# A graph network kernel: the scatters of its result are put behind the last gather of sources in POOL's order

## The chip, the cores and the metric

The kernel runs on one core of a Trainium2 chip. The metric is device microseconds (us) of one execution: the median of several runs, lower is better. Engines are named as the profile names them: PE (matmuls), PEld (its weight loads), DVE (vector), ACT (scalar), POOL and SP. POOL and SP also issue DMA transfers; each engine takes its instructions in the order in which they stand in its own queue.

## What is computed

Two layers of a graph network over 6250 nodes with 128 features and 206250 edges, each with a residual and a layer norm. Here is the reference cut to its frame:

```python
x = layernorm(x + L0(x))      # 5 rounds of h = segment_sum(h[col] * w, row), then a linear layer
x = layernorm(x + L1(x))      # attention of every node over its incoming edges:
#   k, v  = (x[src] * (edge_sh @ Wang.T)) @ Wlin * (relu(edge_attr @ W1 + b1) @ W2)
#   alpha = <q[dst] Wdot, k> per head;  attn = softmax of alpha over the edges of one dst
#   L1    = segment_sum(attn * v, dst) @ Wout
```

The second layer is the part that the change touches.

## The kernel before

The first part of the program sorts and counts edges and runs the five rounds of the first layer as matmuls with a matrix of counts (`propagate`). It leaves the first layer's result twice in DRAM: `x1_d` in the order of nodes, and `x1_r` in the order of rank, where nodes are ranked by how many edges they have. That makes 49 tiles of 128 nodes each, and tile `t` needs at most `WIDTHS[t]` edges per node: 64 for the first tile, 22 for the last, 1658 in all.

`attend` (line 709) is the second layer. A tile's edges are taken as columns: column `j` holds edge `j` of each of its 128 nodes. Up to four columns make a group, and there are 433 groups. For a group:

- `fetch` (line 764) brings in what it needs. For each column one indirect DMA, issued from POOL (line 782), gathers the 128 source rows of 512 bytes from `x1_d` into the tile `xs`; `xs` has six buffers, one per group. SP's queue loads edge data (`ea`, line 775) and, once per tile, the nodes' own rows (`x1s`, line 768).
- `turn`, `nets`, `radial` and `keys` (lines 806 to 870) are the compute: transposes of `xs` (line 811) and matmuls on PE, copies out of PSUM on ACT, products on DVE.
- After a tile's last group, `softmax` (line 872) runs as a generator. It is stepped a little at a time between the groups that follow, and ends with the tile's result `z[:, t, :]` and its mean and variance.
- After the tiles numbered 12, 25, 38, 45, 47 and 48 (`NORMS`, line 47) the layer norm of all tiles since the last such point is finished: one DVE instruction per tile (line 927) and behind it one indirect DMA from POOL (line 931), which scatters the tile's 128 rows to their nodes' places in `out`.

The loop (line 947) goes over `i`, the group now in the nets, and fetches group `i + 3` at its top. The order of PE, DVE and ACT is the order of the program text as it runs (`manual_schedule`, line 946). POOL and SP are not in that list: a planner places their instructions, by its estimates of when their inputs are ready. `declare_no_dep` says that two scatters need not wait for each other. After `attend` the program loads a flag (`flag2`, line 1269) on every engine and, in this case, branches past a general version of the work.

Of the kernel before, what the change touches and what calls it, by code (L numbers as in the profile page):

```python
# [18 lines left out]
P = 128  # L19
N = 6250  # L20
# [123 lines left out]
def stats(nc, work, z, v):  # L144
    st = work.tile([P, nc.vector.BN_STATS_DIM], F32, name="st")
    nc.vector.bn_stats(st, z)
    nc.vector.bn_aggr(v, st)
# [528 lines left out]
def pieces(t):  # L676

    return [(c, OFFS[t] + c * SC, min(SC, WIDTHS[t] - c * SC)) for c in range(-(-WIDTHS[t] // SC))]
# [30 lines left out]
def attend(tc, w1, b1, wang, w2, wlin, wqd, wout, ident, rows, c_iota, src_all, eas_o, x1_d, x1_r, out):  # L709


    nc = tc.nc
    WM = WIDTHS[0]
    with ExitStack() as s:
        one = s.enter_context(tc.tile_pool(name="at1", bufs=1))
# [30 lines left out]
        nc.vector.tensor_scalar(none, degf, 0.0, None, OP.is_equal)  # L746
        z = one.tile([P, NT, D], F32, name="z")
        v = one.tile([P, NT, 2], F32, name="v2")
        puts = []
        kvs = [one.tile([P, WIDTHS[i], DK + D], F32, name=f"kv{i}") for i in range(2)]  # L750

        groups = [(t, j, min(4, w - j)) for t, w in enumerate(WIDTHS) for j in range(0, w, 4)]
# [3 lines left out]
        def ps(name):  # L756
            return pp.tile([P, CH], F32, name=name, tag="ps")
# [6 lines left out]
        def fetch(g):  # L764
            t, j, n = groups[g]
            if j == 0:
                x1s[t] = three.tile([P, D], F32, name="x1s")
                nc.sync.dma_start(x1s[t], x1_r[t * P:(t + 1) * P, :])
            if j % SC == 0:

                c, s, m = pieces(t)[j // SC]
                ea[t, c] = three.tile([P, 4, SC * 32], FR, name="ea")
                for i in range(8):
                    at = (i % 4 // 2) * 32 + i // 4 * 16
                    nc.sync.dma_start(
                        ea[t, c][16 * i:16 * i + 16, :, :m * 32].bitcast(F32),
                        bass.AP(tensor=eas_o.tensor, offset=eas_o.offset + (at * OFFS[NT] + s) * P,
                                ap=[[OFFS[NT] * P, 16], [m * 32, 4], [1, m * 32]]))
            xs[g] = deep.tile([P, 4, D], F32, name="xs")
            for i in range(n):  # L780
                c = OFFS[t] + j + i
                nc.gpsimd.indirect_dma_start(  # L782
                    out=xs[g][:, i, :], out_offset=None, in_=x1_d[:, :],
                    in_offset=bass.IndirectOffsetOnAxis(ap=src_all[:, c:c + 1], axis=0))

        def begin(t):

# [49 lines left out]
        def radial(g):  # L837

            t, j, n = groups[g]
            r = r1.pop(g)  # L840
            p_r = pp.tile([P, 2, CH], F32, name="p_r")
            for i in range(n):
                u = i % 2 * (DK + D)
                nc.tensor.matmul(p_r[:, i // 2, u:u + DK + D], r[:, i, :], w2_s, start=True, stop=True)  # L844
            rr[g] = two.tile([P, 4, DK + D], F32, name="rr")
            r2 = rr[g].rearrange("p (b i) f -> p b (i f)", i=2)
            for b, f in banks(n):
                nc.scalar.copy(r2[:, b, :f], p_r[:, b, :f])  # L848

        def keys(g):  # L850
# [12 lines left out]
            for b, f in banks(n):  # L863
# [5 lines left out]
            nc.vector.tensor_reduce(al[t][:, j:j + n], a[:, :, :DK].rearrange("p j (h k) -> p j h k", h=H),  # L869
                                    AX.X, OP.add)  # L870

        def softmax(t):

            w = WIDTHS[t]
            a = kv[t]
            l = al.pop(t)[:, :w]
            ex = two.tile([P, WM, H], F32, name="ex")
            m = two.tile([P, H], F32, name="m")
            d = two.tile([P, H], F32, name="d")
            nc.vector.tensor_tensor(l, l, keep[t][:, :w, None].to_broadcast([P, w, H]), OP.min)  # L880
            nc.vector.tensor_reduce(m, l.rearrange("p j h -> p h j"), AX.X, OP.max)
            nc.vector.tensor_tensor(l, l, m[:, None, :].to_broadcast([P, w, H]), OP.subtract)
            yield
            nc.scalar.activation(ex[:, :w], l, AF.Exp)
            yield
            nc.vector.tensor_tensor(ex[:, :w], ex[:, :w],
                                    ok[t][:, :w, None].to_broadcast([P, w, H]), OP.mult)
            nc.vector.tensor_reduce(d, ex[:, :w].rearrange("p j h -> p h j"), AX.X, OP.add)
            nc.vector.tensor_scalar(d, d, none[:, t:t + 1], None, OP.add)
            nc.vector.reciprocal(d, d)  # L890
            yield

            for u in range(0, w, 8):
                k = min(8, w - u)
                av = a[:, u:u + k, DK:].rearrange("p j (h f) -> p j h f", h=H)
                nc.vector.tensor_tensor(av, av, ex[:, u:u + k, :, None].to_broadcast([P, k, H, D // H]),  # L896
                                        OP.mult)
                yield
                if u > 0:
                    nc.vector.tensor_add(a[:, :k, DK:], a[:, :k, DK:], a[:, u:u + k, DK:])  # L900
                    yield
            for h in (4, 2, 1):
                nc.vector.tensor_add(a[:, :h, DK:], a[:, :h, DK:], a[:, h:2 * h, DK:])  # L903
            yield
            av = a[:, :1, DK:].rearrange("p j (h f) -> p j h f", h=H)
            o = two.tile([P, H, D // H], F32, name="o")
            nc.vector.tensor_tensor(o, av[:, 0], d[:, :, None].to_broadcast([P, H, D // H]), OP.mult)
            yield
            tr = ps("tr4")
            nc.tensor.transpose(tr[:, :P], o.rearrange("p h d -> p (h d)"), ident)  # L910
            oT = two.tile([P, P], F32, name="oT")
            nc.scalar.copy(oT, tr[:, :P])
            yield
            y = ps("y4")
            nc.tensor.matmul(y[:, :D], oT, wo, start=True, stop=True)
            nc.vector.tensor_add(z[:, t, :], x1s.pop(t), y[:, :D])
            stats(nc, two, z[:, t, :], v[:, t, :])
            if t + 1 in NORMS:
                yield
                t0 = NORMS[NORMS.index(t + 1) - 1]  # L920
                rs = two.tile([P, NT], F32, name="rs")
                n = t + 1 - t0
                nc.vector.tensor_scalar(rs[:, :n], v[:, t0:t + 1, 1], EPS, None, OP.add)
                nc.scalar.activation(rs[:, :n], rs[:, :n], AF.Sqrt)
                nc.vector.reciprocal(rs[:, :n], rs[:, :n])
                for u in range(t0, t + 1):
                    nc.vector.tensor_scalar(z[:, u, :], z[:, u, :], v[:, u, 0:1],
                                            rs[:, u - t0:u - t0 + 1], OP.subtract, OP.mult)

                    k = min(P, N - u * P)  # L930
                    st = nc.gpsimd.indirect_dma_start(
                        out=out[:, :], in_=z[:k, u, :], in_offset=None,
                        out_offset=bass.IndirectOffsetOnAxis(ap=rows[:k, u, 0:1], axis=0)).ins
                    for q in puts:
                        tc.declare_no_dep(st, q, reason="a node has one place in the order")
                    puts.append(st)
                    if u % 4 == 3:
                        yield

# [2 lines left out]
        def step(of):  # L942
            if of and next(of[0], None) is None and of[0].gi_frame is None:
                of.pop(0)

        with tc.manual_schedule(engines=MANUAL):
            for i in range(-3, len(groups) + 1):
                live = [0 <= i + x < len(groups) for x in range(-1, 4)]
                if live[4]:
                    fetch(i + 3)  # L950
                if live[1]:
                    nets(i)
                step(running)
                if live[0]:
                    radial(i - 1)
                if live[2]:
                    turn(i + 1)
                step(running)
                if live[0]:
                    keys(i - 1)  # L960
                    t, j, n = groups[i - 1]
                    if j + n == WIDTHS[t]:
                        running.append(softmax(t))
                if len(running) > 1:
                    step(running)
                if live[3] and groups[i + 2][1] == 0:
                    begun.append(begin(groups[i + 2][0]))
                step(begun)
            for r in running:
                for _ in r:  # L970
                    pass


def attend_any(tc, w1, b1, wang, w2, wlin, wqd, wout, c_heads, c_sum, ident, last, srct, dstt, eat,
# [375 lines left out]
```

## Time and profile before

| | us |
|---|---|
| median of 3 runs | 4537.38 (4534.1 to 4539.81) |
| the profiled execution, its own time | 4539.91 |
| its span in the trace | 4538.1 |
| first gather of line 782 starts | 2248.5 |
| first scatter of line 931 starts | 3049.5 |
| last gather of line 782 starts | 4489.4 |
| last scatter of line 931 starts | 4525.3 |

Between 2248 and 4490 us, a stretch of 2242 us, the engines' busy times are PE 1934.84, PEld 1770.90, DVE 1931.95, ACT 893.28 and POOL 1721.02 us, with a granted PE clock of 0.96 of full speed and the DMA engines busy for 0.53 of the time.

How to read the profile: a busy time is the sum of the durations of an engine's instructions, and leaves out the instructions that only handle registers, branches and semaphores. A line "L782" is line 782 of the kernel. In a group of instructions the first number after the bar is the busy time, the second the mean duration of one in ns, and after the second bar stands how long the engine idled just before these instructions and what ended most of that idle time ("issue" is time in which the engine waited for nothing that the profile shows). In a wait, the three numbers are the total, the number of times and the longest.

### The profile page before, as it was taken

Reading aid. Unit: us, or ns where it says so; the run is one execution under the profiler, and the core shown is the slowest. Engines: PE = TensorE matmul, PEld = TensorE weight load, DVE = VectorE, ACT = ScalarE, POOL = GpSimd, SP = SyncE. Lnnn points to the kernel's source line nnn. Section 1 sums busy time; section 2 is a strip of 40 time slices with the busy share of each in tenths; the row PEclk is TensorE's granted clock in tenths of the full one; section 3 lists DMA queues with packets and bytes.
Section 4 is the critical chain, followed back from the end, with each engine's and each line's share of the span. In section 5 each row is a group of like instructions: output and inputs, shape, how many; then the busy total and the mean of one; then the engine's idle time right before and its main releaser. Section 6 shows DMA issues by size and latency. Waiting matters only on the chain.

```text
span 4538.1 us, 73113 instructions
## 1 busy us (share of the span) xinstructions
PE 3783.3 (83%) x24823; PEld 3370.0 (74%) x24823; DVE 3762.0 (83%) x6000; ACT 2045.8 (45%) x4137; POOL 2361.9 (52%) x2339
## 2 busy tenths in 40 slices
PE   4455666988999999999698888988888878888886
PEld 4455555877888888887488888877878878787775
DVE  9899997757877778766479888997888979898897
ACT  0156665545556565554243434443434434444343
POOL 0350000264333434312477777777777777777774
PEclk9966777999999999999899999999999999999998
DMA  9033335557777788755365555554555555555442
GB/s 325 11 81 80 79 80 139 139 145 217 230 230 220 224 248 239 229 154 161 102 111 102 100 103 105 101 98 97 101 99 102 100 106 98 105 104 102 93 101 46
DMA packets 389736, 601.64 MB, mean 133 GB/s; under 512 B 120093, under 2 KB 325205, under 8 KB 378554
## 3 DMA queue, kind: packets, MB, share of 16 engines
q1 hardware_dynamic: 255930, 356.57, 32.4%
q0 software_dynamic: 127056, 204.67, 19.8%
q10 hardware_dynamic: 6368, 35.63, 2.3%
q8 instruction: 201, 3.29, 0.3%
q14 instruction: 181, 1.48, 0.1%
HBM read 491.89 MB, written 132.25 MB: 138 GB/s over the span
## 4 chain that ended last, share of the span: by engine, by line
PE 22%; DVE 10%; DMA 8%; POOL 8%; issue 6%; ACT 1%; SPq 0%; POOLq 0%; DVEq 0%; ACTq 0%
DMA xs<-x_d,src_all 8%; POOL xs L782 7%; PE p_r L844 6%; PE p_k L860 5%; PE p_k L858 3%; PE acc L438 3%; DVE mkv L833 3%; DVE kv L865 3%; PE p_g L825 2%; PE p_x L811 1%; DVE kv L896 1%; PE p_h L825 1%; DVE kv L903 1%; DVE kv L867 1%; POOL x_r L362 1%
## 5 line engine op out<-in xcount | busy, mean ns | idle before, releaser
L782 POOL DMA_INDIRECT xs<-x_d,src_all x1658 | 1674.0, 1010 | 507.0 <-issue 431.3
L438 PE MATMUL acc<-c,parts 128*128 128x512 f32 (+1 forms) x6370 | 1410.0, 382 | 53.9 <-DVE c L421 40.0
L438 PEld LDWEIGHTS acc<-c,parts 128*128 128x128 f32 x6370 | 1154.1, 189 | 280.0 <-DVE c L421 44.9
L421 DVE CAST c<-c 128x1024 fp32r<-128x1024 uint8 x980 | 683.6, 716 | 251.6 <-PE acc L438 186.4
L860 PE MATMUL p_k<-wlin_s,mkv 128*128 128x128 f32 x3316 | 756.5, 311 | 0.0
L434 ACT CAST c<-c 128x512 fp32r<-128x512 uint8 x735 | 454.8, 621 | 559.2 <-PE acc L438 434.6
L858 PE MATMUL p_k<-wlin_s,mkv 128*128 128x64 f32 x3316 | 582.5, 259 | 66.7 <-DVE kv L865 65.7
L844 PE MATMUL p_r<-w_s,r 128*128 128x192 f32 x3316 | 618.9, 329 | 0.0
L858 PEld LDWEIGHTS p_k<-wlin_s,mkv 128*128 128x128 f32 x3316 | 524.4, 199 | 96.8 <-DVE kv L865 96.0
L844 PEld LDWEIGHTS p_r<-w_s,r 128*128 128x128 f32 x3316 | 569.1, 193 | 34.0 <-ACT rr L848 0.2
L865 DVE TENSOR_TENSOR kv<-rr,p_k 128x768 f32<-128x768 f32 (+2 forms) x443 | 396.7, 897 | 205.8 <-PE p_k L860 189.8
L848 ACT COPY rr<-p_r 128x768 f32<-128x768 f32 (+2 forms) x443 | 334.8, 758 | 475.0 <-PE p_r L844 465.0
L833 DVE TENSOR_TENSOR mkv<-p_g,xT 128x512 f32<-128x512 f32 (+3 forms) x866 | 533.9, 658 | 7.1 <-PE p_g L825 6.7
L860 PEld LDWEIGHTS p_k<-wlin_s,mkv 128*128 128x128 f32 x3316 | 524.6, 199 | 0.0
L827 ACT ACTIVATE r<-p_h,b_s 128x512 f32<-128x512 f32 (+3 forms) x433 | 289.9, 670 | 461.4 <-PE p_h L825 454.7
L223 PE MATMUL p_c<-oh_h,oh_l 128*128 128x100 bf16 x3136 | 301.2, 273 | 214.8 <-DVE oh_h L153 214.8
L662 POOL DMA_DIRECT2D eas_o<-eT_l x252 | 204.1, 813 | 504.7 <-DVE eT_l L656 490.4
L223 PEld LDWEIGHTS <-oh_l 128*128 128x128 bf16 x3136 | 289.5, 124 | 223.5 <-DVE oh_h L153 216.9
L811 PE MATMUL p_x<-ident,xs 128*128 128x128 f32 x1658 | 277.0, 279 | 130.8 <-DMA xs<-x_d,src_all 123.8
L225 ACT CAST cT<-p_c 128x500 uint8<-128x500 f32 (+1 forms) x637 | 306.3, 638 | 61.3 <-DVE c_row L231 61.2
L811 PEld LDWEIGHTS p_x<-ident,xs 128*128 128x128 f32 x1658 | 212.5, 142 | 163.4 <-DMA xs<-x_d,src_all 127.5
L814 ACT COPY xT<-p_x 128x512 f32<-128x512 f32 (+3 forms) x433 | 247.9, 573 | 136.8 <-PE p_x L811 134.0
(195 smaller groups left out, 4533.7 us busy)
## 6 DMA issues: line engine op xcount, KB each, us to landing
c<-counts SPq DMA_DIRECT2D x360, 384.0 KB
ea<-eas_o SPq DMA_DIRECT2D x648, 128.0 KB
c<-counts SPq DMA_DIRECT2D x120, 448.0 KB
eas_o<-eT_l POOLq DMA_DIRECT2D x162, 256.0 KB
counts<-c_row SPq DMA_DIRECT2D x582, 48.0 KB
xs<-x_d,src_all POOLq DMA_INDIRECT x1658
eat<-in_eas ACTq DMA_DIRECT2D x1, 25792.0 KB
counts<-c_row SPq DMA_DIRECT2D x194, 56.0 KB
```

Of the source, the lines that this page charges most:

```text
L223: nc.tensor.matmul(p_c[:, q - q0], oh_los[t % 2][:, q // Q, :, q % Q], oh_hi[:, q // Q, :, q % Q], start=True, stop=True)
L421: nc.vector.tensor_copy(c[:, u:u + 1024].rearrange("p (n b x) -> p n b x", n=2, b=2), r[:, :, v:v + 512].rearrange("p b (n x) -> p n b x", ...
L434: nc.scalar.copy(c[:, 1024:w].rearrange("p (b x) -> p b x", b=2), r[:, :, 512:])
L438: nc.tensor.matmul(a[:, :v - u], parts[:, j, i, :], c[:, u:v], start=(j == 0 and i == 0), stop=(j == NT - 1 and i == 1))
L782: nc.gpsimd.indirect_dma_start(out=xs[g][:, i, :], out_offset=None, in_=x1_d[:, :], in_offset=bass.IndirectOffsetOnAxis(ap=src_all[:, c:c ...
L811: nc.tensor.transpose(p_x[:, i * P:(i + 1) * P], xs[g][:, i, :], ident)
L833: nc.vector.tensor_tensor(mkv[g][:, i, :n].rearrange("p j (b e) -> p b j e", b=4), p_g[:, i, :n * P].rearrange("p (b j e) -> p b j e", b=4 ...
L844: nc.tensor.matmul(p_r[:, i // 2, u:u + DK + D], r[:, i, :], w2_s, start=True, stop=True)
L848: nc.scalar.copy(r2[:, b, :f], p_r[:, b, :f])
L858: nc.tensor.matmul(p_k[:, i // 2, u:u + DK], m[:, 0, i, :], wlin_s[:, :DK], start=True, stop=True)
L860: nc.tensor.matmul(p_k[:, i // 2, u + DK:u + DK + D], m[:, 1, i, :], wlin_s[:, DK:], start=True, stop=True)
L865: nc.vector.tensor_mul(k.rearrange("p (b i) f -> p b (i f)", b=b.stop - b.start), r2[:, b, :f], p_k[:, b, :f])
```

## The change

The scatter leaves `softmax`. There, `done` now only notes that a tile is normed. A new function `store` issues the scatters of all tiles in `done`, each within `tc.issue_after(fetched)`, which gives POOL's order an edge from the instruction `fetched` to each scatter: the scatter stands behind it in the queue, without a semaphore to wait for. `fetched` is what `fetch` returns, the last gather of the group fetched last. `store` is called only from the point in the loop at which no group is left to fetch, and in the loop that runs the remaining generators to their end. The scatters keep their order among themselves, their inputs and their destinations.

```diff
-        puts = []
+        puts, done = [], []
...
-                nc.gpsimd.indirect_dma_start(
+                fetched = nc.gpsimd.indirect_dma_start(
                     out=xs[g][:, i, :], out_offset=None, in_=x1_d[:, :],
-                    in_offset=bass.IndirectOffsetOnAxis(ap=src_all[:, c:c + 1], axis=0))
+                    in_offset=bass.IndirectOffsetOnAxis(ap=src_all[:, c:c + 1], axis=0)).ins
+            return fetched
...
+        def store():
+
+            for u in done:
+
+                k = min(P, N - u * P)
+                with tc.issue_after(fetched):
+                    st = nc.gpsimd.indirect_dma_start(
+                        out=out[:, :], in_=z[:k, u, :], in_offset=None,
+                        out_offset=bass.IndirectOffsetOnAxis(ap=rows[:k, u, 0:1], axis=0)).ins
+                for q in puts:
+                    tc.declare_no_dep(st, q, reason="a node has one place in the order")
+                puts.append(st)
+            done.clear()
...
-                    k = min(P, N - u * P)
-                    st = nc.gpsimd.indirect_dma_start(
-                        out=out[:, :], in_=z[:k, u, :], in_offset=None,
-                        out_offset=bass.IndirectOffsetOnAxis(ap=rows[:k, u, 0:1], axis=0)).ins
-                    for q in puts:
-                        tc.declare_no_dep(st, q, reason="a node has one place in the order")
-                    puts.append(st)
+                    done.append(u)
...
-                    fetch(i + 3)
+                    fetched = fetch(i + 3)
...
+                if i + 3 >= len(groups):
+                    store()
             for r in running:
                 for _ in r:
-                    pass
+                    store()
+                store()
```

## The prediction

> **What bounds the kernel now.** I began with the page's busy row in 40 slices. From slice 20 on, which is about 2248 us and the start of `attend`, PE, PEld and DVE stand at 7 to 9 tenths and POOL at a flat 7. Nothing there is full, so I asked the groups by line what the idle time before POOL's work is.
>
> ```profile
> POOL 0350000264333434312477777777777777777774
> L782 POOL DMA_INDIRECT xs<-x_d,src_all x1658 | 1674.0, 1010 | 507.0 <-issue 431.3
> ```
>
> The gathers of sources (line 782) are busy 1674.0 us, and POOL idled 507.0 us before them: 0.306 us before each of the 1658. That is a fixed gap, not a wait. The timeline of POOL shows it, here at the last block of scatters and on to the end of the program:
>
> ```profile
> 4475.37 0.97 POOL L931 DMA_INDIRECT out<-z,rows  x1 [0.31 <-DMA out<-z,rows]
> 4476.64 0.97 POOL L931 DMA_INDIRECT out<-z,rows  x1 [0.30 <-issue]
> 4477.92 0.99 POOL L782 DMA_INDIRECT xs<-x_d,src_all  x1 [0.30 <-PE p_h L825]
> ...
> 4488.13 0.95 POOL L782 DMA_INDIRECT xs<-x_d,src_all  x1 [0.30 <-issue]
> 4489.39 0.95 POOL L782 DMA_INDIRECT xs<-x_d,src_all  x1 [0.31 <-issue]
> 4511.42 1.10 POOL L931 DMA_INDIRECT out<-z,rows  x1 [21.07 <-DVE z L927]
> 4512.82 0.99 POOL L931 DMA_INDIRECT out<-z,rows  x1 [0.30 <-DVE al L882]
> 4525.33 1.57 POOL L931 DMA_INDIRECT out<-z,rows  x1 [11.51 <-DVE z L927]
> ```
>
> Columns: start, duration, then in brackets the idle time before. Whatever the bracket names, the gap is 0.30. From the first gather (2248.5) to the end of the last (4490.3) POOL issues 1658 gathers and 46 scatters in one unbroken row; three gaps of 1703 are over 0.4 us, the longest 0.94. So POOL never waits for a free `xs` buffer, though only six exist: the compute always keeps up, and **POOL's rate of issue sets the length of the stage**, although its busy share is 7 tenths. The other side of it is PE's waits between 2248 and 4490:
>
> ```profile
> PE p_x L811 <- DMA xs<-x_d,src_all: 123.8, 80, 8.1
> PE p_k L858 <- DVE kv L865: 62.5, 99, 1.6
> ```
>
> PE stood 123.8 us waiting for gathered sources, its largest wait in the stage.
>
> **What is removed from the middle.** 46 scatters (tiles 0 to 45) stand ahead of the last gather, in blocks near 3049, 3663, 4202 and 4466; three come after it. In the groups of the window 2248 to 4491 the 46 are busy 47.2 us with 14.0 us of gaps before them: 61.2 us, 1.33 per slot. With them gone every later gather is issued sooner, and the last one ends at 4490.3 - 61.2 = **4429.2**.
>
> Does the compute follow? Yes, by a comparison inside the trace: between the blocks POOL already runs gathers alone (2300 to 3045, 3085 to 3660, 3700 to 4200, 4235 to 4463), and in each of these PE still waits for sources: 32.1, 32.2, 12.0 and 10.6 us. Those stretches are what the whole stage becomes. SP's loads (`ea`, `x1s`) follow as they do there.
>
> **What is added at the end.** The 46 scatters go behind the last gather, on the same engine and DMA queue. No engine waits for a scatter's landing except the end of the program, so nothing but scatters 47 to 49, the load of `flag2` (0.33 us on POOL's queue) and the end stands behind them. Their data are long there. Price of a slot: 1.33 (the mean of the 46, beside compute) or 1.27 (0.97 + 0.30, the quiet ones). I take 1.33, since half of the train still runs beside the last tiles: 46 x 1.33 = 61.2, so POOL is at 4429.2 + 61.2 = 4490.3. POOL's total work until here is only reordered; the gain is not in it.
>
> **Where the gain is.** It is in the two waits at the end, 21.07 and 11.51 us, in which POOL stands idle for the last tiles' norms. Their compute ends 61.2 us earlier (the norm of tile 48 at 4525.0 - 61.2 = 4463.8, that of 47 at about 4450), before POOL comes to them at 4490.3. So the last three scatters go straight through: 3 x 1.3 = 3.9, last one done at 4494.2. From the end of the last scatter to the end of the span before: 4538.1 - (4525.33 + 1.57) = 11.2 us, unchanged (landing, drains, the branch on `flag2`). Sum: 4494.2 + 11.2 = 4505.4 against 4538.1, **32.7 us less**. As a check, the two waits add up to 32.6.
>
> What is late next: POOL itself, by 26 us over the compute. The rest of the edit (a returned value, a list) is no instruction.
>
> The profiled execution took 4539.9 us (span 4538.1 and 1.8 around it), the median of the three runs is 4537.4. The difference, not the absolute, is carried over: 4537.4 - 32.7 = **4504.7 us**.
>
> **A rule that speaks against it.** The Trainium skill, "DMA: Bandwidth & Descriptors", Rules for kernel authors, advises to issue a DMA early so that its fixed cost lies beside compute; its section on the anatomy of one DMA puts a DMA from this queue at about 2.0 us plus bytes over 436e3 per us. Here stores are deferred. A scatter moves 128 x 512 B = 64 KB, so by that rule an exposed one is 2.15 us (an estimate), and 49 of them one after another 105.4. By the rows, 13 of them in one run (3663.4 to 3679.2) start 1.31 us apart: the 2 us is a landing that overlaps with the next issue, and is paid once, inside the 11.2. The row decides.
>
> **The rivals.**
> 1. *A slower train.* The scatters of `x1_r` (line 362), of the same 64 KB, averaged 1.228 + 0.304 = 1.53 us while DVE worked hard beside them: 49 x 1.53 = 75.0, end 4429.2 + 75.0 + 11.2 = 4515.4, gain 22.7, time **4514.7**. For it: single scatters there took 2 to 3.4 us. Against: in `attend` none of the 46 took over 1.46, and after 4464 DVE has nothing left to do.
> 2. *Slower than before: the train's length is exposed at the landing price.* If the writes of 49 scatters back up, so that each slot costs what a whole DMA does (2.15), the end is 4429.2 + 105.4 + 11.2 = 4545.8, 7.7 later: **4545.1**. It decides from (4526.9 - 4429.2) / 49 = 1.99 us per slot. For it: the 49 gathers of line 178, also in one train, took 1.867 + 0.306 = 2.17 each. Against: those began at 1.25 and slowed only as DVE's work came beside them, and the longest run of scatters here shows no rise from its first to its thirteenth.
> 3. *The compute takes the place of POOL.* The pauses of 61.2 us also let PE catch up: in the windows round the four blocks PE waits for sources 11.7 + 10.4 + 9.0 + 2.8 = 33.9 us, so up to 27.3 us of the pauses was work. If POOL had to wait that long for `xs` buffers instead, everything behind comes 27.3 later, gain 5.4, time **4532.0**. Against: the lag of compute behind the gathers stays at one or two groups of the six that fit, before a block as well as after one.
> 4. *It doesn't do what it says*: the order doesn't bind, or a late tile's scatter is planned into the train and holds it up. If nothing moves, **4537.4**. For the first nothing speaks: the named instruction is whatever gather was fetched last when the scatters are traced.
>
> **How the numbers follow.** Forecast 73 in 100, slower train 10, backed-up train 8, compute-bound 6, no effect 3. A measurement of this kernel tells about 0.2%, 9 us, from no change. Faster: 73 + 10 + half of rival 3 = 86; within: the other half and rival 4 = 6; slower: 8. Range: the low end is the train at 1.27 (49 x 1.27 = 62.2: 4502.6 in the span, 4501.9 in time) and half of the 11.2 us tail gone, 4496; the high end takes in rival 1 and some 4 us for a longer drain, 4519. Left outside are rivals 2 to 4 and a few per cent of the rest.
>
> **What would show it.** In POOL's timeline: no scatter among the gathers, the last gather ending near 4429, then a train of 49 at 1.27 to 1.35 each; the two waits on the norm (32.6 us) gone from POOL's rows; the last norm on DVE about 4464, then DVE, PE and ACT idle for some 30 us; PE's waits for sources down from 123.8 to some 60 to 90. Wrong, if gaps before line 782 exceed 0.3 in number (compute-bound), if slots in the train near 2 us (landing), or if a scatter in the train still waits for a norm.

## The result, and the profile after

| | before | after |
|---|---|---|
| median, us | 4535.74 (4 runs, 4530.4 to 4539.81) | 4508.31 (4 runs, 4502.95 to 4512.36) |
| the profiled execution: span | 4538.1 | 4510.6 |
| first gather starts | 2248.5 | 2256.3 |
| last gather ends | 4490.3 | 4433.3 |
| last norm (tile 48) starts on DVE | 4524.7 | 4476.7 |
| last scatter ends | 4526.9 | 4500.5 |

The ratio is 0.9939, with a 95% interval of 0.9922 to 0.9957: 27.4 us less between the medians, where 32.7 were forecast and the interval allows 20 to 35. The predicted time was 4504.7 us.

Here are the lines of the page after the change that answer to those shown of before: POOL's row of busy tenths and the group of the gathers (busy, mean ns, idle before them).

```profile
POOL 0350000164333343303277777777777777777777
L782 POOL DMA_INDIRECT xs<-x_d,src_all x1658 | 1672.0, 1008 | 505.4 <-issue 428.2
```

The 4 in the last slice has become a 7: POOL is at work to the end. The idle time before the gathers, 505.4 us, is again 0.305 per gather, so nothing new holds them up. The timeline of POOL (start, duration, idle before) shows where the last gather passes into the train, and the end of the train:

```profile
4431.13 0.95 POOL L782 DMA_INDIRECT xs<-x_d,src_all  x1 [0.30 <-PE tr L925]
4432.39 0.95 POOL L782 DMA_INDIRECT xs<-x_d,src_all  x1 [0.30 <-issue]
4433.65 1.00 POOL L879 DMA_INDIRECT out<-z,rows  x1 [0.30 <-issue]
4434.95 1.00 POOL L879 DMA_INDIRECT out<-z,rows  x1 [0.30 <-issue]
...
4466.43 1.83 POOL L879 DMA_INDIRECT out<-z,rows  x1 [0.30 <-DMA out<-z,rows]
...
4496.43 0.97 POOL L879 DMA_INDIRECT out<-z,rows  x1 [0.31 <-issue]
4497.70 0.97 POOL L879 DMA_INDIRECT out<-z,rows  x1 [0.30 <-DMA out<-z,rows]
4498.97 1.56 POOL L879 DMA_INDIRECT out<-z,rows  x1 [0.30 <-DMA out<-z,rows]
```

All 49 scatters stand behind the last gather, 0.30 us apart to the very last. The waits of 21.07 and 11.51 us for the last norms are gone: the norm of tile 48 was done at 4477.1, and POOL came to its scatter at 4499.0. PE's largest wait, which was 123.8 us, is 71.0 us between 2248 and 4440:

```profile
PE p_x L812 <- DMA xs<-x_d,src_all: 71.0, 53, 3.7
```

### The profile page after: what moved, and what is told of

It is laid out like the page before. It is cut to its first block, busy times and chain, and to the rows that moved or that the text cites. A ratio compares the mean times of both kernels' runs of the same rounds, so it can differ in the third digit from the quotient of the medians.

```text
span 4510.6 us, 73113 instructions
## 1 busy us (share of the span) xinstructions
PE 3777.1 (84%) x24823; PEld 3365.8 (75%) x24823; DVE 3762.0 (83%) x6000; ACT 2044.0 (45%) x4137; POOL 2360.7 (52%) x2339
## 3 DMA queue, kind: packets, MB, share of 16 engines
q1 hardware_dynamic: 255930, 356.57, 32.6%
## 4 chain that ended last, share of the span: by engine, by line
PE 24%; DVE 12%; DMA 6%; POOL 6%; issue 6%; ACT 1%; SPq 0%; DVEq 0%; POOLq 0%; ACTq 0%
PE p_r L845 6%; DMA xs<-x_d,src_all 6%; POOL xs L782 5%; PE p_k L861 5%; PE p_k L859 4%; DVE mkv L834 3%; DVE kv L866 3%; PE acc L438 3%; PE p_g L826 2%; PE p_x L812 2%; DVE kv L911 1%; DVE kv L918 1%; DVE kv L868 1%; PE p_h L826 1%; POOL x_r L362 1%
## 5 line engine op out<-in xcount | busy, mean ns | idle before, releaser
L782 POOL DMA_INDIRECT xs<-x_d,src_all x1658 | 1672.0, 1008 | 505.4 <-issue 428.2
L859 PEld LDWEIGHTS p_k<-wlin_s,mkv 128*128 128x128 f32 x3316 | 517.1, 197 | 105.9 <-DVE kv L866 105.0
L861 PEld LDWEIGHTS p_k<-wlin_s,mkv 128*128 128x128 f32 x3316 | 517.8, 197 | 0.0
L826 PE MATMUL p_g<-ea,wang_s 128*128 128x512 f32 (+3 forms) x866 | 285.9, 412 | 16.3 <-DVE mkv L834 14.6
```

The source lines that it names most:

```text
L782: fetched = nc.gpsimd.indirect_dma_start(out=xs[g][:, i, :], out_offset=None, in_=x1_d[:, :], in_offset=bass.IndirectOffsetOnAxis(ap=src_a ...
L826: nc.tensor.matmul(o[:, :n * P], wt, e, start=True, stop=True)
L859: nc.tensor.matmul(p_k[:, i // 2, u:u + DK], m[:, 0, i, :], wlin_s[:, :DK], start=True, stop=True)
L861: nc.tensor.matmul(p_k[:, i // 2, u + DK:u + DK + D], m[:, 1, i, :], wlin_s[:, DK:], start=True, stop=True)
```

## The experiments

The theory is that POOL's order sets the end: 46 slots taken out from ahead of the last gather bring the last tile's compute forward, and what is gained is only POOL's idle time at the end, since the slots come back behind it. The first rival is that the gain comes from gathers that run smoothly; then it goes with the number of scatters moved. The second is that the landing of the train costs something of its own, and the third that the compute takes POOL's place.

**How many scatters are moved.** Four kernels ran on one chip (number 1 in the record) against one set of runs of the kernel before (median 4534.77 us, 11 runs). The first is the full change once more.

> The changed kernel itself, beside the others. POOL-order theory: 27 to 35 us less than before (the two waits of 32.6 us for the last norms go, POOL is busy without a gap to its end).

Measured: 4509.24 us, ratio 0.9941 (0.9928 to 0.9953), 25.5 us less, just under the 27 to 35 expected; the interval allows 21 to 33.

The next two bind only the first tiles' scatters, and issue the others where the norm is traced, as before:

```diff
                     done.append(u)
+                    if 13 <= u < 46:      # the other kernel: 26 <= u < 46
+                        done.pop()
+                        put(u)            # the scatter without issue_after
```

> Only the scatters of tiles 0 to 12 go behind the last gather, those of 13 to 45 stay among the gathers. POOL-order theory: 13 slots of 1.33 us are taken out ahead of the last gather, the last tile's compute ends 17 us sooner and still ends after POOL: 17 us less than before, with some 15 us of waiting for the last norms left on POOL. Smoother-compute theory (the gain comes from gathers that are no longer interrupted, so it goes with the number moved): 13/46 of the whole gain, 8 us less.

> The scatters of tiles 0 to 25 go behind the last gather. POOL-order theory: 26 slots of 1.33 us are 34.6 us, as long as the waits at the end, so the whole gain is there already: 31 to 34 us less than before, the same as the full change, though 20 scatters stay among the gathers; last norm and end of POOL's train meet near the same time. Smoother-compute theory: 26/46 of the gain, about 15 us less.

Measured: with 13 moved, 4520.33 us, ratio 0.9969 (0.9956 to 0.9981), 14.4 us less. With 26 moved, 4507.46 us, ratio 0.9937 (0.9925 to 0.9949), 27.3 us less. 26 of the 46 bring the whole gain, and 13 bring half of it: the gain grows with the first slots and is flat from 26 on. The medians lie under the 17 and the 31 to 34 us expected, but their intervals (9 to 20 and 23 to 34 us) hold these values. They don't hold the 8 and 15 us that smoother gathers would have given, the 8 only just.

The end of POOL's timeline with 13 moved:

```profile
4484.53 0.97 POOL L884 DMA_INDIRECT out<-z,rows  x1 [0.30 <-issue]
4487.89 1.07 POOL L884 DMA_INDIRECT out<-z,rows  x1 [2.39 <-DVE z L946]
4489.26 0.97 POOL L884 DMA_INDIRECT out<-z,rows  x1 [0.30 <-DVE al L901]
4501.81 1.56 POOL L884 DMA_INDIRECT out<-z,rows  x1 [11.59 <-DVE z L946]
```

The short train is over before the last two norms, and 14.0 us of waiting for them remain, where 32.6 were (some 15 were expected): the compute still sets the end. With 26 moved the norm of tile 48 starts at 4488.5, and the train comes to its scatter at 4494.2 without a gap; the two ends nearly meet, so the point at which POOL overtakes the compute lies between 13 and 26. With all 46 moved POOL is 22 us behind the norm.

**Without the train.**

```diff
-                    done.append(u)
+                    if u >= 46:
+                        done.append(u)
```

> Leaves out the scatters of tiles 0 to 45, so most of the result isn't written; the three last are behind the last gather. POOL-order theory: the train no longer sets the end, the last norm does (4464 us, then one scatter and 11 us): 61 us less than before, some 28 less than the full change. Smoother-compute theory: the train beside the last tiles costs nothing, so as the full change, about 27 to 33 us less than before. If landing of the train were the cost, more than 28 us would go with it.

Measured: 4476.80 us, ratio 0.9877 (0.9861 to 0.9892), 58.0 us less than before and 32.4 less than the full change beside it. POOL's end there:

```profile
4423.29 0.95 POOL L782 DMA_INDIRECT xs<-x_d,src_all  x1 [0.30 <-issue]
4450.80 1.00 POOL L879 DMA_INDIRECT out<-z,rows  x1 [26.56 <-issue]
4452.10 1.00 POOL L879 DMA_INDIRECT out<-z,rows  x1 [0.30 <-issue]
4464.36 1.56 POOL L879 DMA_INDIRECT out<-z,rows  x1 [11.26 <-DVE z L942]
```

POOL waits for the norms again, so the compute sets the end. The expectation named more than 28 us between the two kernels as the sign of a landing that costs something, and 32.4 is more. Counted from the first gather, the two traces differ by 30.3 us: behind the full train the last scatter ends 27.0 us later, and from there to the end of the span it is 10.1 us (4510.6 - 4500.5) in place of 6.8 (4472.7 - 4465.9). That last stretch took 11.2 us before the change too, where the scatters were spread out. So its length goes with whether the 46 scatters are there, and not with their standing in a row; a landing price of the train isn't seen.

**Two chips on which POOL waits for the compute.** The other eight runs came to two other chips, numbers 5 and 13 in the record, four to each. The kernel before takes 5063 us on the one and 5070 on the other, and the granted PE clock of its profiled execution is 0.87 on both in place of 0.93. First the kernel before, on chip 5:

> The kernel before once more, for a second trace of it: the two waits of POOL for the last norms are 32 to 33 us again whatever the time at which the stage starts; the start of the first gather differs by some us from run to run (2248.5 in the first trace).

```profile
L782 POOL DMA_INDIRECT xs<-x_d,src_all x1658 | 1670.5, 1008 | 970.9 <-issue 431.4
```

This is its group of gathers. They cost what they cost elsewhere (1008 ns), but POOL idles 970.9 us before them in place of 507.0. It now waits for buffers that PE has yet to read: 274.3 us of it end with the transposes of `xs`, and 152.8 us with an event whose sender the view can't name ("remote"). The gathers issued are on average 19.4 columns ahead of the transposes, of 24 that fit into six buffers, where it was 6.3. At the end POOL waits 55.2 us for the last norms. The expectation of 32 to 33 us was missed, and with it the premise.

That the compute is late doesn't mean that one of its engines is full. Here is the same stretch of 900 us in both traces of the kernel before, first from the first result, then from chip 5: the busy times of PE, PEld, DVE, ACT and POOL with the number of instructions, then the PE clock, the busy share of DMA, and GB/s.

```profile
3300.00:4200.00 900.00, 781.22 (x5327) 713.91 (x5328) 792.25 (x1434) 363.97 (x621) 691.11 (x686) 0.97 0.54 102
```

```profile
3300.00:4200.00 900.00, 699.56 (x4386) 636.55 (x4385) 654.18 (x1146) 292.62 (x498) 568.61 (x565) 0.90 0.43 84
```

Every engine is less busy there. What the traces show instead are late starts. In the first trace, each product of line 865 that found DVE idle began at most 0.24 us after the end of the last of its inputs, `p_k` from PE and `rr` from ACT. On chip 5, 109 of the 443 began more than 1 us after it, 368 us in sum. What delays them isn't shown.

The full change ran on chip 13:

> The full change on the chip that this call gets. Where POOL issues without a gap in the second layer before the change, 25 to 28 us less than before. On a chip like that of the last call, where POOL waits before line 782 for the compute (970.9 us of idle time in place of 507.0), the gathers that the change advances only wait longer for buffers: within 12 us of before, and the scatters' train is exposed or not as the last tile's compute lets it be.

Measured: 5055.97 us (12 runs) against 5069.89 (29 runs), ratio 0.9975 (0.9952 to 0.9999), 13.9 us less, about half of the gain on chip 1 and hardly told from none; slightly outside the 12 us expected. The end of its POOL timeline:

```profile
4988.20 0.97 POOL L879 DMA_INDIRECT out<-z,rows  x1 [0.30 <-issue]
5028.97 1.07 POOL L879 DMA_INDIRECT out<-z,rows  x1 [39.80 <-DVE z L942]
5030.34 0.97 POOL L879 DMA_INDIRECT out<-z,rows  x1 [0.30 <-DVE al L897]
5042.90 1.56 POOL L879 DMA_INDIRECT out<-z,rows  x1 [11.58 <-DVE z L942]
```

In the trace of the kernel before from the same chip (below) the stage begins within 0.1 us of this one's. The last gather ends at 4929.5 here and at 5000.5 there, 71 us sooner; the last norm's scatter starts at 5042.9 and 5058.7, 16 us sooner. The 46 slots were taken out as on chip 1, but the compute followed only in small part. The train is over at 4989.2 and POOL waits 51.4 us for the norms. This is the third rival where it holds.

The kernel before on chip 13:

> The kernel before once more, for a second trace. Where POOL sets the pace: waits for the last norms of 32 to 33 us again, 2282 to 2290 us from the first gather to the end, and a start of the first gather that lies within 10 us of 2250.

Measured: 5073.36 us in its one run; first gather at 2296.7, 56.1 us of waits for norms. It bears out the trace from chip 5, and says nothing of chip 1, for which it was meant.

**Fewer buffers.** The pool of `xs` with `bufs=3` in place of 6, in the full change:

> The full change with three buffers for gathered sources in place of six. POOL-order theory: the compute is one or two groups behind the gathers, so three buffers are nearly enough, POOL still shows few gaps above 0.3 us and the time is within 5 us of the full change, about 26 us less than before. Compute-bound theory: the depth is what hides the compute's lag, so POOL waits before line 782 by tens of us and most of the gain is lost.

> Once more the full change with three buffers for sources. Where POOL sets the pace: within 5 us of the full change, and POOL's gaps before line 782 stay near 507 us in all. Compute-bound theory: gaps grow by tens of us and the gain is lost.

Measured: on chip 5 a ratio of 0.9976 (0.9956 to 0.9996), and on chip 13 one of 0.9953 (0.9932 to 0.9974), where six buffers gave 0.9975. POOL's idle time before the gathers was 948.3 us with three buffers and 959.0 with six on chip 13. So half the depth costs nothing that can be seen, even where POOL waits for buffers. For chip 1, which the expectation was about, there is no run.

**What makes a gather slow.** In the trace after, POOL's instructions from 2248 us on mostly take 0.95 us, but 200 of them more than 1.15. Laid beside DVE's timeline, 178 of these 200 overlap the softmax's product `kv<-kv,ex` (line 911), which only 212 of the 1263 under 1.0 us do. One such pair, with the row of POOL first:

```profile
4409.76 1.83 POOL L782 DMA_INDIRECT xs<-x_d,src_all  x1 [0.30 <-issue]
```

```profile
4409.60 1.17 DVE L911 TENSOR_TENSOR kv<-kv,ex 128x1024 f32<-128x1024 f32 x1
4410.69 0.94 DVE L866 TENSOR_TENSOR kv<-rr,p_k 128x768 f32<-128x768 f32 x1
```

The gather lasts 0.88 us longer than a quick one. It begins 0.16 us after a product of 1.17 us and ends 0.82 us after that product's end. This is the rule in the whole trace. 466 of the 1658 gathers begin while a DVE product or sum with both inputs in SBUF has more than 0.15 us to run, and 448 of these end 0.81 to 0.84 us after that instruction's end. 638 begin in the same way within a product whose second input lies in PSUM (such as line 866, of up to 0.95 us) or within a reduction with one input: none of them takes over 0.97 us. So what tells the slow gathers from the quick ones is not the length of the DVE instruction but its two inputs in SBUF. Of the 98 us by which the gathers exceed 0.95 us each, 95 us lie in the 466.

Two kernels change these long DVE instructions. The first cuts the products and sums over 8 columns into two of 4 each:

```diff
-                nc.vector.tensor_tensor(av, av, ex[:, u:u + k, ...
+                for b, n in cuts:        # (0, 4), (4, 4)
+                    nc.vector.tensor_tensor(av_b, av_b, ex[:, u + b:u + b + n, ...
```

> The full change with the softmax's long DVE products and sums over 8 columns (1.2 us each) cut into pieces of 4. In the trace 178 of 200 gathers that took over 1.15 us overlap such a product. If a DVE instruction with two inputs in SBUF holds POOL up until it ends, shorter ones hold it up for less: the gathers' mean falls from 1008 to about 985 ns, 38 us less of POOL's time, against some 60 us more of DVE's own fixed costs: 4475 to 4505 us. If the slow gathers have another cause, the mean stays at 1008 and the time at 4509 or above.

> Once more the full change with the long DVE products cut into pieces of 4. The last call gave gathers of 998 ns in place of 1008 to 1011 and 28 us more of DVE. Where POOL sets the pace: 10 ns x 1658 = 17 us less than the full change, so some 42 us less than before. Where the compute sets it: no gain, as in the last call.

The second replaces the sums over columns by reductions:

```diff
-                    nc.vector.tensor_add(a[:, :k, DK:], a[:, :k, DK:], a[:, u:u + k, DK:])
...
+            for f in range(0, D, 32):
+                nc.vector.tensor_reduce(sv[:, f:f + 32],
+                                        a[:, :w, DK + f:DK + f + 32].rearrange("p j f -> p f j"), AX.X, OP.add)
```

> The full change with the sums over columns (two inputs in SBUF, 266 us of DVE in all) replaced by four reductions with one input each. If two inputs in SBUF are what holds POOL up, the gathers beside these become quick: mean 1008 to about 980 ns, some 45 us less of POOL's time, as far as DVE, with slower strided reductions, keeps up: 4465 to 4505 us. If any long DVE instruction does it, no change in the mean, and 4509 or above.

Both ran only on chips 5 and 13, so their times don't decide what they would bring where POOL sets the pace: the cut gave ratios of 0.9992 (0.9971 to 1.0013) on chip 5 and 0.9983 (0.9966 to 1.0001) on chip 13, no gain, as expected for such a chip; the reductions gave 1.0123 (1.0102 to 1.0144) on chip 5, with reductions of 386.5 us on DVE in place of 266 us of sums. What they do to a gather can be read there, in min, median and max of its duration in ns, first for the full change and then with the cut, both from chip 13:

```profile
L782 POOL DMA_INDIRECT xs<-x_d,src_all x1658: 946/952/2009, 2296.8 to 4928.3; - x185
```

```profile
L782 POOL DMA_INDIRECT xs<-x_d,src_all x1658: 946/952/1496, 2307.9 to 4949.5; - x185
```

The longest gather falls from 2.0 to 1.5 us, about the half of a long product that was cut away, and the median stays. The mean falls from 1010 to 996 ns, and with the reductions to 990 (985 and 980 were expected): 23 and 33 us of POOL's time. That these DVE instructions hold a gather up is borne out by both. The reductions take 2.0 us on the mean, longer than any product, and none of the 310 gathers that begin within a reduction there, with more than 0.15 us of it to run, takes over 0.97 us.

## Why the prediction was right

**What bounds the kernel** was read rightly: POOL's row of equal gaps, not its busy share of 7 tenths. Moving 13 scatters brought 14.4 us, where 13 slots of 1.33 us are 17.3; moving 26 brought the whole gain, and moving 46 no more, as it must be once POOL overtakes the compute.

**The sum.** Counted from the first gather, which removes where the stage happens to start, the forecast for the last gather was 4429.2 - 2248.5 = 2180.7 us, and it was 4433.3 - 2256.3 = 2177.0. The train of 49 was put at 65.0 us (4429.2 to 4494.2) and took 67.2, since three scatters between 4453 and 4470 took 1.70 to 1.94 us beside the last tiles' DVE products. The tail was put at 11.2 and took 10.1. So the three errors are -3.7, +2.2 and -1.1 us, and partly cancel. From first gather to end the profiled executions differ by 2289.6 - 2254.3 = 35.3 us. The remaining 7.8 us go the other way: in this execution the stage began later. The trace after and the four of changed kernels from chip 1 begin it between 2248.7 and 2258.0, though nothing ahead of it was edited, so a spread of some 9 us lies there. Only one trace of before exists at this speed; whether its start at 2248.5 is typical stays open. The medians of the runs say 27.4 and 25.5 us, with intervals that reach 32.7 (20 to 35, and 21 to 33): the forecast lies at their upper edge, and where the missing 5 to 7 us went isn't settled.

**A term that was off, and hidden.** The compute was to end 61.2 us earlier and 34.7 us behind the last gather. It ended 43.7 behind it (4433.3 to 4477.1). With 26 moved it was 35.0 and without the train 39.8. So the pauses had let the compute catch up by some 5 to 9 us, as rival 3 held, in a smaller measure than its bound of 27.3. What the prediction held against that rival, a lag of one or two groups, is right on the mean before the change (6.3 columns), but the lag went up to 13 columns, over three groups. The prediction put POOL 26 us behind the compute, and this margin, measured as 22, covers the error in the full change. Without the train it is in the open. The 58.0 us measured there, where 61 were expected, show too little of it, since the stretch behind the last scatter is 4.4 us shorter in that kernel (6.8 us against 11.2).

**The rule against it** did not decide (the Trainium skill, "DMA: Bandwidth & Descriptors": to issue a DMA early in Rules for kernel authors, and some 2 us for each in its section on the anatomy of one DMA): 49 scatters in a row took 1.37 us each with gap and all, so the price of a landing is not paid per scatter.

**The rivals.** The slower train came in part, 1.37 per slot in place of 1.53. The landing price of 2.15 did not come. Rival 3 was given 6 in 100, and describes chips 5 and 13, which the prediction could not know of. There its own test fires: gaps before line 782 above 0.3 us. Why the compute is so much slower there is not settled. The product `p_k` of 128 x 128 takes 328 ns there in place of 311, 5%, while the stage from the first gather to the end takes 2770.6 us in place of 2289.6, 21%. The late starts shown above go with it; how much of the 21% they make isn't shown.

No kernel tried beats the full change clearly: 26 moved is 1.8 us faster beside it, within the interval.

## What to carry to other kernels

An engine that issues small DMAs can be full at a busy share of 7 tenths: look for equal gaps before its instructions and for the absence of longer ones, and count slots, not busy time. Work that nobody waits for belongs behind the last item that somebody waits for; but it comes back as a tail, so the gain ends where that tail grows as long as the other engines' end, here between 13 and 26 of 46. Such a gain belongs to a bound: where the issuing engine waits for the others, as on chip 13, about half of it is gone.

## What the hardware showed

- An indirect DMA of 128 rows of 512 bytes costs POOL 0.95 us and a fixed gap of 0.30, as a gather and (0.97) as a scatter; 49 scatters in one row show no rise.
- A gather that begins within a DVE product or sum with both inputs in SBUF ends 0.81 to 0.84 us after it (448 of 466 in the trace after), and takes up to 1.95 us; beside products with an input in PSUM, and beside reductions of 2.0 us, it takes 0.95. This cost POOL some 95 us in the second layer, and on chip 13 halving the products took the longest gather from 2.0 to 1.5 us.
- The same program took 4535 us on chip 1, 5063 on chip 5 and 5070 on chip 13. On the slower two POOL waits for the compute in the second layer, though no engine is fuller there: PE was busy for 78% of a stretch of 900 us on chip 5, and for 87% of it in the first trace.
